# Turning attention probabilities by DMA instead of on TensorE, with each attention spread over two sets of products

## The chip, the cores and the metric

The kernel runs on one core of one Trainium2 chip. The metric is the device time of one execution, in microseconds (us). TensorE (PE) multiplies matrices into PSUM, VectorE (DVE), ScalarE (ACT) and GpSimd (POOL) work elementwise, and SyncE (SP) issues every DMA of this kernel. Each engine runs its own instructions in the order in which the program issued them, and waits on semaphores for the others.

## The reference

Input `x` is 128 graphs of 64 nodes with 768 features, with a boolean 64x64 mask per graph. Two layers follow one another, each `x = layernorm(x + f(x, adj))`, all in float32.

```python
# layer 0: 12 heads of 64, additive attention, gate
h = einsum('bnd,ade->bane', x, W); th = tanh(h)
attn = leaky(th @ w_src + swap(th @ w_dst)); masked softmax
feat = elu(attn @ h + b); gate = sigmoid(x @ H_w.T + H_b)
f0 = gate * feat + (1 - gate) * x
# layer 1: 6 heads of 128, dot-product attention
q, k, v = heads(x @ Wq + bq), heads(x @ Wk + bk), heads(x @ Wv + bv)
probs = softmax(q @ k.T / sqrt(128) + bias(adj))
f1 = merge(probs @ v) @ Wf + bf
```

The change is in layer 1, in what stands between `probs` and `probs @ v`.

## The kernel before, in words

**Tiles.** A tile is 128 rows, that is two graphs. 64 tiles make 32 pairs, and 16 groups of two pairs (four tiles). A weight of 768x768 is cut in 2x2 blocks, and a product of two 2x2 block matrices is done with seven block products (a `Job`, lines 199 to 247): `product(i)` issues three matrix products of 128 rows into a PSUM bank, and `way_out(i)` evicts or adds the bank. `step` (L257) issues the product of one step and then the ways out of the step before it. Some products accumulate onto a bank that an earlier way out has to have read first: 6, 7, 4 and 3 do (L212), which follows from the seven-product scheme.

**Stages.** The first half of the program (up to L977) does layer 0 and also layer 1's values `v`, which go to DRAM (`v_d`), as do the layer's result by rows (`x1_d`) and by features (`x1T_d`). The second half (from L980) goes over 16 groups. In each group there are three sets of query and key products, one for each feature column `fc` of 128 (two heads: `fc` and `fc + 3`), and then the output products of the group before. A set is 14 steps in the order `WOVEN` (L46), two jobs interleaved. Query and key steps have 256 columns, output steps 384.

**The order of the work around the change.** It is written out by hand with generators. `woven` (L513) issues a step and then advances each side generator by one `yield`; `drain` runs a generator to its end. `attention` (L345) is one such side: it loads values (eight DMAs, L354), and then, `yield` by `yield`: scores on PE into a bank `sp` (L366), bias and maximum on DVE (L375, L383), subtraction (L385) and exponential on ACT (L386), row sum and division on DVE (L390 to L393), the transposes on PE into a bank `sT` (L398), their copy into `scT` on ACT (L403), context products on PE into two banks `cp` (L414), and their eviction by ACT into `ctxT` (L427). The attention of `(g, fc)` is created after set `(g, fc)` and advanced in the next set, where it ends. PSUM banks with the tag `m` (scores, transposes, context products) number two. Other sides are `residuals` (L436: loads `x1_d`, adds the bias on POOL and forms the block sums of `ctxT` on DVE), `finish` (L497: layer norm and output of the pairs two output sets back) and, in the first group, `last_weight` (L986: the output weight's four blocks, and their sums on DVE). `load_group` (L300) loads the next group's `x1T_d` blocks and forms their four sums on POOL; it is called after the third set of each group.

**PE** needs, in a query or key job, that ACT (ways out of products 1, 6, 7 and 4, L338 and L340) and DVE (products 2, 7 and 3, L339) have read the bank. In output jobs all ways out are on DVE (L481).

Of the kernel before, what the change touches and what calls it, by code (L numbers as in the profile page):

```python
# [8 lines left out]

F32 = mybir.dt.float32  # L10
U8 = mybir.dt.uint8
AF = mybir.ActivationFunctionType
ALU = mybir.AluOpType
AX = mybir.AxisListType

P = 128
# [3 lines left out]
HK = KC // 2  # L20
# [11 lines left out]
GT = 4  # L32
# [58 lines left out]
def kernel(  # L91
# [21 lines left out]
    nc = tc.nc  # L113
# [13 lines left out]
    def bank(tag, name, bufs=2):  # L127
        return ps.tile([P, 512], F32, tag=tag, name=name, bufs=bufs)
# [3 lines left out]
    x1T_d = [dram.tile([P, KC, PAIR * P], F32, name=f"x1Td_{p}") for p in range(NP)]  # L132
    v_d = [dram.tile([P, D], F32, name=f"vd_{t}") for t in range(2 * NP)]
    dst_d = [dram.tile([P, H0], F32, name=f"dstd_{t}") for t in range(2 * NP)]


    ident = const.tile([P, P], F32, name="ident")
# [157 lines left out]
    def query_tiles(g, fc):  # L295
        qk[g, fc] = [
            pools["early"].tile([P, 2, GT * P], F32, tag=f"{k}T", name=f"{k}T_{g}_{fc}") for k in "qk"
        ]

    def load_group(g, eng, between=lambda: None):  # L300

        pool = pools["early"]
        sums = sum_tiles(pool, "sq", W2, f"q{g}")
        between()
        blocks = {}
        for m, kh in ((0, 0), (1, 0), (1, 1), (0, 1)):
            t = pool.tile([P, HK, W2], F32, tag=f"a{m}{kh}", name=f"a{m}{kh}_{g}", bufs=1)
            nc.sync.dma_start(out=t, in_=x1T_d[2 * g + m][:, kh * HK : (kh + 1) * HK, :])
            blocks[m, kh] = t
        groups[g], steps = block_sums(eng, sums, *(blocks[m, kh] for m in range(2) for kh in range(2)))  # L310
        return steps

    def feature_jobs(g, fc):
# [28 lines left out]

    ctxT = {}

    def attention(g, fc, bias):  # L345

        sb = pools["late"]
        qT, kT = qk.pop((g, fc))

        v = sb.tile([P, GT, 2, E1], F32, tag="v1", name=f"v1_{g}_{fc}")  # L350
        for a in range(2):
            c0 = (a * J1 + fc) * E1
            for i in range(GT):
                nc.sync.dma_start(  # L354
                    out=v[a * N : (a + 1) * N, i, :, :],
                    in_=v_d[GT * g + i][:, c0 : c0 + E1].rearrange("(g m) e -> m g e", m=N),
                )
        yield
        yield
        yield  # L360
        sp = bank("m", f"sp_{g}_{fc}")
        for i in range(GT):
            for a in range(2):
                for gr in range(2):
                    at = slice(i * P + gr * N, i * P + (gr + 1) * N)
                    T.matmul(  # L366
                        sp[gr * N : (gr + 1) * N, (i * 2 + a) * N : (i * 2 + a + 1) * N],
                        qT[:, a, at],
                        kT[:, a, at],
                        start=True,  # L370
                        stop=True,
                    )
        yield
        sc = sb.tile([P, GT, 2, N], F32, tag="sc", name=f"sc_{g}_{fc}")
        V.tensor_tensor(  # L375
            sc,
            sp.rearrange("p (i a m) -> p i a m", i=GT, a=2),
            bias.unsqueeze(2).to_broadcast([P, GT, 2, N]),
            ALU.add,
        )  # L380
        sc3 = sc.rearrange("p i a m -> p (i a) m")
        mx = small.tile([P, 2 * GT], F32, tag="mx1", name=f"mx1_{g}_{fc}")
        V.tensor_reduce(mx, sc3, AX.X, ALU.max)  # L383
        yield
        V.tensor_tensor(sc3, sc3, mx.unsqueeze(2).to_broadcast([P, 2 * GT, N]), ALU.subtract)  # L385
        S.activation(sc, sc, AF.Exp, scale=SCALE)  # L386
        yield
        yield
        den = small.tile([P, 2 * GT], F32, tag="den1", name=f"den1_{g}_{fc}")
        V.tensor_reduce(den, sc3, AX.X, ALU.add)  # L390
        rden = small.tile([P, 2 * GT], F32, tag="rden1", name=f"rden1_{g}_{fc}")
        V.reciprocal(rden, den)
        V.tensor_tensor(sc3, sc3, rden.unsqueeze(2).to_broadcast([P, 2 * GT, N]), ALU.mult)  # L393
        yield
        yield
        sT = bank("m", f"sT_{g}_{fc}")
        for i in range(GT):
            T.transpose(  # L398
                sT[:, i * P : (i + 1) * P], sc[:, i].rearrange("p a m -> p (a m)"), ident
            )  # L400
        yield
        scT = sb.tile([P, GT * P], F32, tag="scT", name=f"scT_{g}_{fc}")
        S.copy(scT, sT)  # L403
        yield
        yield
        cp = [bank("m", f"cp_{g}_{fc}_{a}") for a in range(2)]
        for i in range(GT):
            for gr in range(2):
                at = slice(i * P + gr * N, i * P + (gr + 1) * N)
                for a in range(2):  # L410
                    rows = slice(a * N, (a + 1) * N)
                    for half in range(2):
                        e = slice(half * N, (half + 1) * N)
                        T.matmul(  # L414
                            cp[a][e, at], v[rows, i, gr, e], scT[rows, at], start=True, stop=True
                        )
        yield
        if g not in ctxT:
            ctxT[g] = [
                sb.tile([P, KC, W2], F32, tag="ctxT", name=f"ctxT_{g}_{pr}", bufs=4)  # L420
                for pr in range(2)
            ]

        for a in range(2):
            hd = a * J1 + fc
            for pr in range(2):
                S.activation(  # L427
                    ctxT[g][pr][:, hd, :],
                    cp[a][:, pr * W2 : (pr + 1) * W2],
                    AF.Identity,  # L430
                    bias=bias_c["v"][:, hd : hd + 1],
                )
# [80 lines left out]
    def woven(pair, *sides, order=WOVEN):  # L513

        for k, i in order:
            step(pair[k], i)
            for s in sides:
                next(s, None)

    def drain(*sides):  # L520
        for s in sides:
# [458 lines left out]
    with ExitStack() as ph:  # L980
        sb = pools["late"] = ph.enter_context(
            tc.tile_pool(name="sb1", bufs=2, reuse_waits="tile")
        )
        nothing = iter(())

        def last_weight():  # L986

            weights["f"] = load_weight(wf, "wc", "wf")
            pools["bf"] = sb.tile([P, D], F32, name="bf_bc", bufs=1)
            nc.sync.dma_start(out=pools["bf"], in_=bf.partition_broadcast(P))  # L990
            for s in weight_sums(V, weights["f"]):
                for _ in range(3):
                    yield
                s()

        adjs[0] = load_adj(sb, 0, GT, "adjg_0")
        biases = {0: mask_bias(0)}
        attend, done = attention(0, 0, biases[0]), nothing
        next(attend)
        for g in range(NG):  # L1000
            last = g == NG - 1
            rows = residuals(g - 1, False) if g > 0 else last_weight()
            for fc in range(HK):
                if (g, fc) == (0, 0):
                    continue
                if fc == 1 and not last:
                    adjs[g + 1] = load_adj(sb, GT * (g + 1), GT, f"adjg_{g + 1}")
                if fc == 2 and not last:
                    biases[g + 1] = mask_bias(g + 1)
                if (g, fc) == (0, 1):  # L1010
                    pair, order = (jobs["Q"], jobs["K"]), LAST_REST
                else:
                    query_tiles(g, fc)
                    pair, order = feature_jobs(g, fc), WOVEN
                sides = [attend] + [done] * (fc == 0) + [rows] * (fc == 2)
                woven(pair, *sides, order=order)
                drain(*sides)
                attend = attention(g, fc, biases[g])
                next(attend)
            if not last:  # L1020
                all_of(load_group(g + 1, G))
            if g > 0:
                pair = out_job(2 * g - 2), out_job(2 * g - 1)
                if last:
                    attend = chain(attend, residuals(g, True))
                woven(pair, *[attend] * (1 + last))
                drain(attend)
                attend = nothing
                done = finish(2 * g - 2, 2 * g - 1)
        p = 2 * NG - 2  # L1030
        pair = out_job(p), out_job(p + 1)
        woven(pair, done, done, order=ENDS[:9])
        drain(done)
        done = finish(p)
        woven(pair, done, done, order=ENDS[9:-1])
        n0, n1 = norm(p + 1, 0), norm(p + 1, 1, last_half=0)
        step(pair[1], ENDS[-1][1])
        next(n0)
        next(n1)
        drain(done)  # L1040
        flush()
        next(n0, None)
        next(n1)
        next(n1, None)
# [42 lines left out]
```

## Time and profile before

| | |
|---|---|
| median of 3 runs | 2967.19 us (2966.39 to 2970.22) |
| profiled execution, its own time | 2970.77 us |
| its span, first to last instruction | 2969.0 us |
| PE busy in the span | 2925.2 us, 99% |
| DVE, ACT, POOL busy | 1796.9, 1009.0, 811.1 us |
| granted TensorE clock | 0.995 |
| one group of layer 1 (2089.96 to 2180.46 in the trace) | 90.50 us, PE busy 90.50 |

The profile is of one execution. "Busy" is the time in which an engine worked on data; the issuing of DMAs is not counted in it. A line of the groups names the line of the kernel, the engine, the operation, what it writes and reads, the shape, the count, then busy us and mean ns of one, and the idle time before it with what ended it. A line of the timeline gives the start and the length in us, the engine and the instruction. PE's matmuls overlap, so what one costs in a stream is read from start to start.

### The profile page before, as it was taken

What the parts mean: (1) busy time and instruction counts of PE and PEld (TensorE: products, weight loads), DVE (VectorE), ACT (ScalarE), POOL (GpSimd) and SP (SyncE); (2) the same over time, 40 slices, a digit from 0 to 9 for tenths busy, and PEclk for the clock granted to TensorE, in tenths of its full rate; (3) what the DMA queues carried; (4) which work ended last, traced back from release to release, by engine and by line L of the source; (5) the groups of instructions that cost most, each with busy time, mean ns of one, the idle gap of its engine ahead of it and who ended that gap; (6) DMA issues with size and microseconds to landing.
All of it is one profiled execution on the core that took longest, in us unless ns stands there. A gap on an engine that the chain in (4) does not pass through costs nothing.

```text
span 2969.0 us, 45314 instructions
## 1 busy us (share of the span) xinstructions
PE 2925.2 (99%) x18048; PEld 2023.0 (68%) x18048; DVE 1796.9 (61%) x3017; ACT 1009.0 (34%) x1761; POOL 811.1 (27%) x650
## 2 busy tenths in 40 slices
PE   7999999999999999999999999999999999999999
PEld 4566666666666666666578777787777887777875
DVE  6878888788788878887844344333343443443345
ACT  2344344444443444444422222222222222222221
POOL 2434333333343333333422212211111212121121
PEclk9999999999999999999999999999999999999999
DMA  5333333334333333343532211222212222112221
GB/s 171 122 109 114 107 121 115 103 118 128 104 119 104 121 113 106 115 129 103 176 97 77 70 60 55 86 86 76 68 52 64 86 76 73 59 57 82 87 80 48
DMA packets 179681, 284.81 MB, mean 96 GB/s; under 512 B 46736, under 2 KB 113296, under 8 KB 179472
## 3 DMA queue, kind: packets, MB, share of 16 engines
q1 hardware_dynamic: 179472, 281.93, 29.1%
q8 instruction: 143, 2.34, 0.3%
q14 instruction: 66, 0.54, 0.1%
HBM read 167.81 MB, written 101.06 MB: 91 GB/s over the span
## 4 chain that ended last, share of the span: by engine, by line
PE 94%; DVE 3%; DMA 1%; ACT 1%; issue 0%; SPq 0%; POOLq 0%; POOL 0%; DVEq 0%; ACTq 0%
PE y_k L222 8%; PE y_o L222 8%; PE y_q L222 8%; PE y_v L222 8%; PE y_h L222 8%; PE y_g L222 8%; PE z_v L222 4%; PE z_o L222 4%; PE z_k L222 4%; PE z_h L222 4%; PE z_q L222 4%; PE z_g L222 4%; PE x_k L222 2%; PE x_o L222 2%; PE x_q L222 2%; PE x_h L222 2%
## 5 line engine op out<-in xcount | busy, mean ns | idle before, releaser
L789 POOL TENSOR_TENSOR x<-gate,x 128x768 f32<-128x768 f32 x64 | 117.4, 1835 | 323.8 <-ACT gate L840 309.0
L457 POOL TENSOR_TENSOR y<-y,bf_bc 128x768 f32<-128x768 f32 x64 | 115.3, 1832 | 311.4 <-DMA y<-x1d 311.4
L481 DVE TENSOR_TENSOR y<-y_o,y 128x384 f32<-128x384 f32 x128 | 71.4, 557 | 202.1 <-PE y_o L222 198.0
L339 DVE TENSOR_TENSOR kT<-z_k,kT 128x256 f32<-128x256 f32 x96 | 40.8, 425 | 239.3 <-PE z_k L222 136.1
L662 POOL TENSOR_TENSOR th<-th,wsd 128x768 f32<-128x768 f32 x64 | 117.2, 1832 | 182.5 <-DVE th L661 182.5
L274 POOL TENSOR_TENSOR rs_b<-ve_b,minus_half 128x1 f32<-128x1 f32 x64 | 35.1, 548 | 452.5 <-DVE ve_b L272 451.7
L192 POOL TENSOR_TENSOR sq_q<-a,a 128x768 f32<-128x768 f32 x16 | 29.2, 1828 | 432.8 <-PE y_o L222 286.9
L222 PE MATMUL y_h<-w_wq,xT 128*128 128x384 f32 x384 | 136.3, 492 | 8.6 <-DMA w_wq<-in_w_dram 7.9
L222 PE MATMUL y_k<-a,hw_wk 128*128 128x256 f32 x576 | 144.6, 387 | 0.0
L222 PE MATMUL y_q<-a,w_wq 128*128 128x256 f32 x576 | 140.9, 381 | 1.9 <-ACT qT L338 1.9
L222 PE MATMUL z_v<-wv,sv_v 128*128 128x384 f32 x384 | 138.9, 498 | 3.2 <-DVE v L652 3.2
L222 PE MATMUL y_q<-sq_q,w_wq 128*128 128x256 f32 x576 | 140.3, 380 | 0.9 <-ACT qT L338 0.9
L222 PE MATMUL y_h<-w_wq,sx_x 128*128 128x384 f32 x384 | 136.5, 492 | 4.2 <-ACT h L622 4.2
L222 PE MATMUL z_q<-sq_q,w_wq 128*128 128x256 f32 x576 | 140.1, 379 | 0.0
L222 PE MATMUL y_k<-sq_q,hw_wk 128*128 128x256 f32 x576 | 140.1, 379 | 0.0
L222 PE MATMUL z_k<-sq_q,hw_wk 128*128 128x256 f32 x576 | 140.0, 379 | 0.0
L338 ACT ACTIVATE qT<-y_q,bq_c 128x256 f32<-128x256 f32 x144 | 67.4, 469 | 213.2 <-PE y_q L222 213.2
L222 PE MATMUL y_v<-wv,sv_v 128*128 128x384 f32 x384 | 136.6, 492 | 3.0 <-DVE sv_v L193 3.0
L386 ACT ACTIVATE sc<-sc 128x512 f32<-128x512 f32 x48 | 30.2, 630 | 319.3 <-DVE sc L385 319.3
L222 PE MATMUL z_h<-w_wq,sx_x 128*128 128x384 f32 x384 | 137.6, 495 | 0.9 <-DVE w_wq L168 0.9
L222 PE MATMUL y_g<-hw_wk,sx_x 128*128 128x384 f32 x384 | 134.9, 488 | 2.4 <-DVE hw_wk L171 2.2
L222 PE MATMUL y_v<-wv,x1T 128*128 128x384 f32 x384 | 136.1, 491 | 1.2 <-ACT x1T L739 1.0
(171 smaller groups left out, 6678.1 us busy)
## 6 DMA issues: line engine op xcount, KB each, us to landing
x<-in_x_dram SPq DMA_DIRECT2D x64, 384.0 KB, 3.6
dd<-dstd SPq DMA_DIRECT2D x128, 192.0 KB, 3.4
x1d<-x SPq DMA_DIRECT2D x64, 384.0 KB, 2.6
x1Td<-x1T SPq DMA_DIRECT2D x32, 768.0 KB, 4.8
vd<-v SPq DMA_DIRECT2D x64, 384.0 KB, 2.9
a<-x1Td SPq DMA_DIRECT2D x64, 384.0 KB, 3.6
v<-vd SPq DMA_DIRECT2D x384, 64.0 KB, 2.3
y<-x1d SPq DMA_DIRECT2D x64, 384.0 KB, 4.1
```

The source lines that it names most:

```text
L192: lambda: e.tensor_tensor(s1, a21, a22, ALU.add),
L222: T.matmul(to[:, : self.n], lhsT, rhs, start=kc == 0 and not more, stop=kc == HK - 1, skip_group_check=more,)
L274: G.tensor_tensor(rstd, ve, minus_half, ALU.pow)
L338: lambda mn, bk_: S.activation(at(*mn), bk_, AF.Identity, bias=bias(mn[1])),
L339: lambda mn, bk_: V.tensor_tensor(at(*mn), bk_, at(*mn), ALU.add),
L386: S.activation(sc, sc, AF.Exp, scale=SCALE)
L457: G.tensor_tensor(y, y, pools["bf"], ALU.add)
L481: V.tensor_tensor(at(*mn), b, at(*mn), ALU.add)
L662: G.tensor_tensor(th[:, 1, :], th[:, 1, :], wsd[:, 1, :], ALU.mult)
L789: G.tensor_tensor(xp, st[t]["gate"], xp, ALU.mult)
```

## The change

All attentions of layer 1 but the last no longer turn their probabilities on PE. A float32 word is taken as two 16-bit halves. ACT copies the low halves and the high halves of the probabilities apart into `scT`'s memory; a DMA stores both to DRAM (`halves_d`, two buffers that take turns); two DMA transposes, one for each half, read them back turned into the memory of `sc`; and ACT joins the halves again into `scT`. The last attention still transposes on PE.

The new steps have more `yield`s between them, so an attention is advanced over two sets: its scores, softmax and the start of the DMAs in the first, the joining copies, context products and their evictions in the second (`older` and `attend` in the loop). The output set and the first query/key set of the next group thus carry the second halves of attentions that the sets before began.

Other edits go with it. The output weight's blocks are loaded two steps apart, and their sums come after the loads. Three of group 1's `x1T_d` blocks are loaded with them, ahead of `load_group`. Two of group 1's four sums go to DVE, and these sums are a side of the next set.

```diff
+    halves_d = [dram.tile([2, GT, P, P], U16, name=f"halvesd_{i}") for i in range(2)]
...
+    of_x1T = {}
+
+    def load_x1T(g, m, kh):
+        t = pools["early"].tile([P, HK, W2], F32, tag=f"a{m}{kh}", name=f"a{m}{kh}_{g}", bufs=1)
+        nc.sync.dma_start(out=t, in_=x1T_d[2 * g + m][:, kh * HK : (kh + 1) * HK, :])
+        of_x1T[g, m, kh] = t
...
-        blocks = {}
         for m, kh in ((0, 0), (1, 0), (1, 1), (0, 1)):
-            t = pool.tile([P, HK, W2], F32, tag=f"a{m}{kh}", name=f"a{m}{kh}_{g}", bufs=1)
-            nc.sync.dma_start(out=t, in_=x1T_d[2 * g + m][:, kh * HK : (kh + 1) * HK, :])
-            blocks[m, kh] = t
-        groups[g], steps = block_sums(eng, sums, *(blocks[m, kh] for m in range(2) for kh in range(2)))
+            if (g, m, kh) not in of_x1T:
+                load_x1T(g, m, kh)
+        groups[g], steps = block_sums(eng, sums, *(of_x1T.pop((g, m, kh)) for m in range(2) for kh in range(2)))
...
-    def attention(g, fc, bias):
+    def attention(g, fc, bias, by_dma=True):
...
-        yield
-        yield
-        sT = bank("m", f"sT_{g}_{fc}")
-        for i in range(GT):
-            T.transpose(
-                sT[:, i * P : (i + 1) * P], sc[:, i].rearrange("p a m -> p (a m)"), ident
-            )
-        yield
         scT = sb.tile([P, GT * P], F32, tag="scT", name=f"scT_{g}_{fc}")
-        S.copy(scT, sT)
-        yield
-        yield
+        if by_dma:
+            yield
+            apart, turned = (
+                t.bitcast(U16).rearrange("p (h e) -> p h e", h=2)
+                for t in (scT, sc.rearrange("p i a m -> p (i a m)"))
+            )
+            words, wordsT = (
+                t.bitcast(U16).rearrange("p (e h) -> p h e", h=2)
+                for t in (sc.rearrange("p i a m -> p (i a m)"), scT)
+            )
+            for h in range(2):
+                S.copy(apart[:, h], words[:, h])
+            yield
+            dr = halves_d[(g * HK + fc) % 2]
+            nc.sync.dma_start(
+                out=dr.rearrange("h i p c -> p h i c"),
+                in_=apart.rearrange("p h (i c) -> p h i c", c=P),
+            )
+            yield
+            yield
+            yield
+            for h in range(2):
+                nc.sync.dma_start_transpose(
+                    out=turned[:, h], in_=dr[h].rearrange("i p c -> (i p) c")
+                )
+            yield
+            yield
+            yield
+            for h in range(2):
+                S.copy(wordsT[:, h], turned[:, h])
+            yield
+            yield
+            yield
+            yield
+            yield
+        else:
...
+    def in_turn(steps):
+        yield
+        for s in steps:
+            s()
+            yield
...
-            weights["f"] = load_weight(wf, "wc", "wf")
+            weights["f"] = load_weight(wf, "wc", "wf", ())
             pools["bf"] = sb.tile([P, D], F32, name="bf_bc", bufs=1)
+            for block in (B11, B21, B22, T3):
+                yield
+                yield
+                load_block(wf, weights["f"], block)
+            load_x1T(1, 0, 0)
+            load_x1T(1, 0, 1)
+            load_x1T(1, 1, 0)
             nc.sync.dma_start(out=pools["bf"], in_=bf.partition_broadcast(P))
             for s in weight_sums(V, weights["f"]):
-                for _ in range(3):
-                    yield
+                yield
                 s()
...
-        attend, done = attention(0, 0, biases[0]), nothing
+        attend, older, done = attention(0, 0, biases[0]), nothing, nothing
...
-                sides = [attend] + [done] * (fc == 0) + [rows] * (fc == 2)
-                woven(pair, *sides, order=order)
+                sides = [older] + [done] * (fc == 0) + [rows] * (fc == 2)
+                woven(pair, *sides, attend, order=order)
                 drain(*sides)
-                attend = attention(g, fc, biases[g])
+                older, attend = attend, attention(g, fc, biases[g], not (last and fc == 2))
                 next(attend)
             if not last:
-                all_of(load_group(g + 1, G))
+                sums = load_group(g + 1, G if g else (V, G))
+                if g:
+                    all_of(sums)
+                else:
+                    done = in_turn(sums)
             if g > 0:
                 pair = out_job(2 * g - 2), out_job(2 * g - 1)
                 if last:
                     attend = chain(attend, residuals(g, True))
-                woven(pair, *[attend] * (1 + last))
-                drain(attend)
-                attend = nothing
+                woven(pair, older, *[attend] * (1 + last))
+                drain(older)
+                if last:
+                    drain(attend)
+                older, attend = attend, nothing
```

More of the change, by code (lines that the diff above doesn't have):

```diff
@@ L11 @@
 U8 = mybir.dt.uint8
+U16 = mybir.dt.uint16
 AF = mybir.ActivationFunctionType
@@ L393, in attention @@
         V.tensor_tensor(sc3, sc3, rden.unsqueeze(2).to_broadcast([P, 2 * GT, N]), ALU.mult)
-        yield
-        yield
-        sT = bank("m", f"sT_{g}_{fc}")
-        for i in range(GT):
-            T.transpose(
-                sT[:, i * P : (i + 1) * P], sc[:, i].rearrange("p a m -> p (a m)"), ident
-            )
-        yield
-        scT = sb.tile([P, GT * P], F32, tag="scT", name=f"scT_{g}_{fc}")
-        S.copy(scT, sT)
-        yield
-        yield
+        scT = sb.tile([P, GT * P], F32, tag="scT", name=f"scT_{g}_{fc}")
+        if by_dma:
[3 more added lines that the diff above has]
+                for t in (scT, sc.rearrange("p i a m -> p (i a m)"))
+            )
+            words, wordsT = (
[30 more added lines that the diff above has]
+            yield
+            sT = bank("m", f"sT_{g}_{fc}")
+            for i in range(GT):
+                T.transpose(
+                    sT[:, i * P : (i + 1) * P], sc[:, i].rearrange("p a m -> p (a m)"), ident
+                )
+            yield
+            S.copy(scT, sT)
+            yield
+            yield
         cp = [bank("m", f"cp_{g}_{fc}_{a}") for a in range(2)]
@@ L518, in woven @@
                 next(s, None)
+    def in_turn(steps):
+        yield
+        for s in steps:
+            s()
+            yield
     def drain(*sides):
@@ L986, in last_weight @@
         def last_weight():
-            weights["f"] = load_weight(wf, "wc", "wf")
+            weights["f"] = load_weight(wf, "wc", "wf", ())
             pools["bf"] = sb.tile([P, D], F32, name="bf_bc", bufs=1)
+            for block in (B11, B21, B22, T3):
+                yield
+                yield
+                load_block(wf, weights["f"], block)
+            load_x1T(1, 0, 0)
+            load_x1T(1, 0, 1)
+            load_x1T(1, 1, 0)
             nc.sync.dma_start(out=pools["bf"], in_=bf.partition_broadcast(P))
             for s in weight_sums(V, weights["f"]):
-                for _ in range(3):
-                    yield
+                yield
                 s()
```

## The prediction

> **What bounds the kernel now.** I read the page's busy shares and chain first, then the groups of layer 1 by form, then PE's, DVE's and SP's timelines over one group of four tiles, then the waits.
>
> ```profile
> PE 2925.2 (99%) x18048; PEld 2023.0 (68%) x18048; DVE 1796.9 (61%) x3017; ACT 1009.0 (34%) x1761; POOL 811.1 (27%) x650
> ...
> PE 94%; DVE 3%; DMA 1%; ACT 1%; issue 0%; SPq 0%; POOLq 0%; POOL 0%; DVEq 0%; ACTq 0%
> ```
>
> PE is busy 99% and carries 94% of the chain. A busy PE alone proves little, so I look at a stretch: one whole group (an output set, then three query/key sets), and inside it the second query/key set.
>
> ```profile
> 2089.96:2180.46 90.50, 90.50 (x638) 70.62 (x637) 35.99 (x79) 22.92 (x46) 16.48 (x12) 1.00 0.22 71
> ...
> 2138.03:2159.16 21.13, 21.13 (x185) 18.22 (x184) 6.84 (x13) 6.39 (x14) 7.13 (x4) 1.00 0.38 119
> ```
>
> The columns are the length, then PE, PEld, DVE, ACT and POOL busy, the clock, the DMA share, GB/s. PE has no gap in 90.5 us and the full clock; ACT works 22.9 us of it, DVE 36.0, DMA 22%. So here a PE instruction that goes is time that goes, if nothing else gets late. PE's timeline around the part that is removed:
>
> ```profile
> 2148.37 1.46 PE L222 MATMUL y_q<-sq_q,w_wq 128*128 128x256 f32 x6
> 2149.66 1.46 PE L222 MATMUL z_k<-sq_q,hw_wk 128*128 128x256 f32 x6
> 2150.96 0.60 PE L398 MATMUL sT<-ident,sc 128*128 128x128 f32 x4
> 2151.40 1.46 PE L222 MATMUL y_k<-sq_q,hw_wk 128*128 128x256 f32 x6
> ```
>
> From start to start a step costs 1.295 us and the four transposes 0.44 (the printed 0.60 overlaps the next). In the output set they cost 0.44 as well (2108.49 to 2108.93). What DVE and ACT spend around them:
>
> ```profile
> 2147.43 0.69 DVE L393 TENSOR_TENSOR sc<-sc,rden 128x512 f32<-128x512 f32 x1
> ...
> L427 ACT ACTIVATE ctxT<-cp,bv_c 128x256 f32<-128x256 f32 x164 | 64.4, 475 | 138.8 <-PE cp L414 138.8
> ...
> L403 ACT COPY scT<-sT 128x512 f32<-128x512 f32 x42 | 24.6, 586 | 151.5 <-PE sT L398 151.5
> ```
>
> Probabilities are ready 10.09 us after that set's start. Layer 1's two own PE waits stand at its beginning, and the DMA rows price the new transfers:
>
> ```profile
> PE y_q L222 <- ACT qT L338: 2.8, 2, 1.9
> ...
> PE x_q L222 <- DMA a<-x1Td: 1.9, 1, 1.9
> ```
>
> ```profile
> vd<-v SPq DMA_DIRECT2D x64, 384.0 KB, 2.9
> ...
> v<-vd SPq DMA_DIRECT2D x384, 64.0 KB, 2.3
> ...
> adjg<-in_adj_dram SPq DMA_DIRECT2D x16, 32.0 KB, 2.2
> ```
>
> **What the Trainium skill says.** "VectorE: DVE Perf Modes", The three transpose paths, gives 390 ns on TensorE and 1309 ns on the DMA crossbar for one 128x128 two-byte block. Here TensorE's four float32 blocks cost 0.44 us together in a stream, so that is a latency and not a rate; no crossbar transfer is in this trace. "DMA: Bandwidth & Descriptors", Latency and other measured facts, gives an effective 261 GB/s for DMA transposes in one kernel. The same page, Two DMAs through the same engine are not ordered, says that a transfer that reads what another wrote has to wait for its completion; so SP will stand at each transpose until the store has landed.
>
> **The change, part by part.** One attention is 4 tiles and one feature column; there are 48, and all but the last go the new way: 47.
>
> *Removed.* 47 x 4 transposes on PE: 47 x 0.435 = **-20.4 us** on the path that sets the end. Also 47 `scT` copies on ACT (0.586 each), off the path.
>
> *Added on ACT.* Two copies that part the halves and two that join them. Halves are 512 two-byte elements per partition; the nearest row is the 512-element copy, 0.586. Net +3 x 0.586 = 1.76 us per attention, 83 in all, or 5.3 per group beside ACT's 22.9 of 90.5. Hidden in ACT's idle time; what matters is who queues behind them. The parting copies come at step 8 behind the division (10.09 us; step 8 starts at 10.35 with the scores' 1.28), so ACT barely waits; behind them is the eviction of step 8's product, wanted at step 11, 3.9 us after step 8 starts, against 1.17 + 0.47. Covered. If two-byte strided copies took twice 0.586 it still fits.
>
> *Added DMAs.* Per attention one store of 256 KB in 1024 runs of 256 bytes, and two transposes of 128 KB. The store lies between the 384 KB row (2.9 us) and something slower for its short runs; adjg's 512 runs of 64 bytes land in 2.2. I take 3.0 (2.5 to 4). The pair of transposes is not in the trace. Low end: a small transfer's landing, 2.2 us. High end: eight 128x128 blocks one after another by the page's price, 10.5 us. An estimate from the page's 261 GB/s: 262,144 bytes take 1.0 us, with 2.3 for the landing of a small DMA and 0.6 for SP's second issue (eight v loads take SP 5.1 to 6.0 us), **3.9 us**, which I take, since blocks of one instruction should overlap. Store and pair: 6.9 us.
>
> *What waits.* ACT's joining copies stand at step 1 of the next set, in front of that set's evictions. PE's step 5 accumulates on a bank that the first eviction must have read. I split the group's sets: a query/key set is 18.13 us bare (the window 2119.90 to 2138.03), and 1.28 more with each of scores and context products.
> - First attention of a group (second half in a set with scores): the division ends at 10.09 of 19.41 us; step 5 starts at 4 x 1.295 + 1.28 = 6.46, less 0.47 for the eviction and 1.17 for joining: 4.82. The room is 9.32 + 4.82 - 1.17 (parting) = **13.0 us** for store and pair.
> - Third (first half in the output set of 29.5 us, division at 15.04 + 1.28): 13.2 + 3.54 - 1.17 = **15.6**.
> - Second (second half in the output set, where no ACT eviction feeds PE, so only the context products at step 6 count): 8.9 + 12.9 - 2.3 = **19.5**.
>
> 6.9 fits all of them with 6.1 us to spare. The cover is the half set of block products; without it each late microsecond is one on PE, 16 times for the first kind.
>
> *SP's queue.* Three more issues per attention, some 0.6 us each. Behind the transposes, where SP stands for the store, are eight v loads (used a set later), four y loads (before issued at 2145.85, now about 2160, landed by 2165, four POOL additions of 1.83 till 2173, wanted from 2180) and the x1T loads (two were issued at 2162.17, now about 2183; landing 3.6, four POOL sums 7.3, done 2194; wanted near 2210). All late, none too late.
>
> *Start of layer 1.* The weight blocks are issued apart, their sums come at step 10 and not 4, three x1T blocks come early, and two of group 1's sums go to VectorE. That aims at both waits above: 0.9 us of the first at 1559 and 1.9. Against it, 3.8 MB are in flight while the second attention's store and transposes want to pass, and the second sum is wanted at the next set's step 5. I take -1.5 (from -2.8 to +3).
>
> *The end.* In the last output set the context products of two attentions follow one another in step 6 with two PSUM banks of that tag: the second waits for four evictions, 1.57 us. **+1.6**, once. I see no cover for it.
>
> *Context products moved, masks, residual sums:* same work at another step, nothing.
>
> **Sum.** -20.4 - 1.5 + 1.6 = -20.3. The profiled execution took 2970.77 us (span 2969.0), so 2950.5 there; it lies 3.6 over the median of the runs, 2967.19, against which I forecast **2946.9 us**. The likeliest case's own range is 2941 to 2953.
>
> **Rivals.**
> - *The transposes are late* (ends slower). [...] If store and pair take over 13.0 us, ACT stands at step 1 of the third query/key set and PE stops at step 5. The gain is gone at 20.4/16 = 1.3 us over, 14.3 us (pair 11.3 with a store of 3.0). The page's block price, 10.5, gives a total of 13.5: over by 0.5, 8 us, still faster. A quarter more than it (13.1 us, total 16.1) gives 3.1 x 16 + 0.5 x 15 = 57 us: **3004 us**. For it: short runs on both sides, the HBM round trip twice. Against: 22% DMA share and 6 us of room.
> - *Partly hidden*: transposes make their neighbours late (v, y and x1T loads behind them on SP) or evictions slip by some tenths in each set. Half of the gain: **2957 us**. For it: PE runs without any gap, so any slip shows. Against: the listed rooms.
> - *No difference*: a pair near 11 us eats the gain just up, **2966 us**.
> - *The DMA path is not what it says*: it could be that the copies go through more work than one pass; at most ACT's 83 us, inside its idle time, so this has no own time.
>
> **How the numbers follow.** Hidden 0.53, partly hidden 0.15, no difference 0.05, late 0.27. Faster by over 0.2% is 0.68, within 0.2% 0.05, slower 0.27; 0.2% (5.9 us) is about what a measurement of this kernel can tell from no change. A range that leaves out 2 in 10 runs from 2940 (under it only if the start gains fully) to 2990, which holds the smaller half of the late cases; 2941 to 2953 stands beside it for the likeliest.
>
> **What would show it.** Right: an output-to-output period of 90.5 - 3 x 0.435 = 89.2 us with PE without gap, no `sT` but in the last attention, joining copies on ACT that start at once in step 1, the two waits at 1559 and 1574 smaller. Late: PE waits on ACT's `qT` in the third query/key set of each group, ACT on a DMA into `sc`. Partly: short PE waits on `ctxT`, `kT` or `y`. The prediction is wrong if the pair takes over 11 us, if a transpose holds SP so long that the x1T sums come late, or if PE spends the removed 0.44 us elsewhere.

## The result and the profile after

The changed kernel takes 3004.78 us (median of 4 runs, 3001.74 to 3011.7); the kernel before, run beside it, 2968.68. The ratio is 1.0126, with a 95% interval of 1.0113 to 1.0138: slower by 36 us, where 20 us less had been forecast. The profiled execution took 3001.74 us, with a span of 2999.9.

The page of the changed kernel first: the busy shares and the chain.

```profile
PE 2915.2 (97%) x17860; PEld 2007.5 (67%) x17860; DVE 1886.1 (63%) x3019; ACT 1095.7 (37%) x1902; POOL 830.3 (28%) x648
...
PE 88%; DVE 8%; ACT 2%; DMA 1%; SPq 1%; issue 0%; POOL 0%; POOLq 0%; DVEq 0%; ACTq 0%
```

PE is busy for 10 us less than before (2925.2), and the span is 30.9 us longer: PE now stands idle for 84.7 us, 40.9 more than before. DVE's busy time has grown by 89 us, though DVE was given nearly the same instructions (3019 instead of 3017). DVE's share of the chain went from 3% to 8%. So something made DVE's instructions longer.

PE's waits in layer 1 (the view of waits from 1535 us on; columns: who waited for whom, us in all, how often, longest):

```profile
PE y_q L225 <- ACT qT L346: 33.3, 20, 2.2
PE y_q L225 <- DVE sq_q L196: 8.3, 1, 8.3
PE cp L460 <- ACT ctxT L473: 1.3, 2, 0.9
```

Of the first, 15 are waits of some 2 us, one in the third set of each group but group 0, and five are short ones (0.2 to 0.6 us) in the same sets. The other two lines are the start and the end of layer 1. One group in windows: from output set to output set, and below it the third query/key set alone.

```profile
2103.70:2196.15 92.45, 89.72 (x626) 69.29 (x625) 43.34 (x79) 28.66 (x56) 18.01 (x12) 1.00 0.28 87
...
2172.18:2196.15 23.97, 21.24 (x182) 17.67 (x181) 15.97 (x20) 7.81 (x18) 8.21 (x4) 1.00 0.35 104
```

The group takes 92.45 us; the mean of 13 groups is 92.19 (from 1642.65 to 2841.06), where before it was 90.50. The first two query/key sets have the forecast 19.41 us. The third should have 20.69 (19.41 and 1.28 for the context products that it also carries) and has 23.97, with PE busy 21.24. Its timeline on PE:

```profile
2182.42 1.56 PE L225 MATMUL z_q<-sq_q,w_wq 128*128 128x256 f32 x6
2184.56 1.56 PE L225 MATMUL y_q<-sq_q,w_wq 128*128 128x256 f32 x6 [0.58 <-ACT qT L346]
2185.96 1.46 PE L225 MATMUL z_k<-sq_q,hw_wk 128*128 128x256 f32 x6
2187.25 1.46 PE L225 MATMUL y_k<-sq_q,hw_wk 128*128 128x256 f32 x6
2190.86 1.56 PE L225 MATMUL y_q<-a,w_wq 128*128 128x256 f32 x6 [2.15 <-ACT qT L346]
```

There are two waits for an eviction by ACT, of 0.58 and 2.15 us; from start to start they cost 3.1 (2.14 in place of 1.40, and 3.61 in place of 1.295). What held ACT, in ACT's timeline:

```profile
2189.30 1.14 ACT L416 COPY scT<-sc 128x512 uint16<-128x512 uint16 x2 [2.97 <-DVE sc L401]
2190.34 0.47 ACT L346 ACTIVATE qT<-y_q,bq_c 128x256 f32<-128x256 f32 x1
```

The parting copies waited 2.97 us for DVE's division, and the eviction that PE needed stood behind them. And what held DVE, in DVE's timeline with POOL's one line of that stretch:

```profile
2178.09 0.69 DVE L391 TENSOR_REDUCE mx<-sc 128x8 f32<-128x512 f32 x1
...
2179.25 2.00 DVE L196 TENSOR_TENSOR so_o<-so_o,ctxT 128x384 f32<-128x384 f32 x1
2181.18 2.30 DVE L393 TENSOR_TENSOR sc<-sc,mx 128x512 f32<-128x512 f32 x1
2183.40 2.17 DVE L197 TENSOR_TENSOR so_o<-ctxT 128x384 f32<-128x384 f32 x1
2185.49 2.16 DVE L198 TENSOR_TENSOR so_o<-ctxT,so_o 128x384 f32<-128x384 f32 x1
2187.57 0.67 DVE L398 TENSOR_REDUCE den<-sc 128x8 f32<-128x512 f32 x1
...
2188.52 0.69 DVE L401 TENSOR_TENSOR sc<-sc,rden 128x512 f32<-128x512 f32 x1
...
2179.03 8.21 POOL L503 TENSOR_TENSOR y<-y,bf_bc 128x768 f32<-128x768 f32 x4 [35.45 <-DMA y<-x1d]
```

Four DVE instructions with two inputs in SBUF (L196, L393, L197 and L198) take 8.6 us. In the kernel before, the same four of a third set take 2.3:

```profile
2166.47 0.68 DVE L385 TENSOR_TENSOR sc<-sc,mx 128x512 f32<-128x512 f32 x1
2167.07 0.55 DVE L193 TENSOR_TENSOR so_o<-so_o,ctxT 128x384 f32<-128x384 f32 x1
2167.54 0.55 DVE L194 TENSOR_TENSOR so_o<-ctxT 128x384 f32<-128x384 f32 x1
...
2169.57 0.55 DVE L195 TENSOR_TENSOR so_o<-ctxT,so_o 128x384 f32<-128x384 f32 x1
```

The slow ones lie exactly beside POOL's four additions of the output bias to the residual rows. These additions were in the second set before, after that set's division. Here is POOL's line of the kernel before:

```profile
2149.37 7.13 POOL L457 TENSOR_TENSOR y<-y,bf_bc 128x768 f32<-128x768 f32 x4 [19.25 <-DMA y<-x1d]
```

The set there ran from 2138.03 to 2159.16. What moved the additions is seen on SP. Before:

```profile
2139.77 5.99 SPq L354 DMA_DIRECT2D v<-vd  x8
2145.85 1.96 SPq L450 DMA_DIRECT2D y<-x1d  x4
```

And after, with the second set running from 2152.77 to 2172.18:

```profile
2164.12 0.40 SPq L419 DMA_DIRECT2D halvesd<-scT  x1
2166.77 2.45 SPq L427 DMA_TRANSPOSE sc<-halvesd  x2
2169.31 6.09 SPq L362 DMA_DIRECT2D v<-vd  x8
2175.44 2.02 SPq L496 DMA_DIRECT2D y<-x1d  x4
```

SP issues its DMAs in the order of the program. The y loads now stand behind the store (which waits for ACT's copies), the transposes (which wait for the store) and eight v loads. They are issued 22.7 us after the second set's start, where it was 7.8 before.

The Trainium skill names such a collision. "SBUF — State Buffer", Who interferes with whom, says that a DVE instruction with two SBUF inputs contends with a GpSimd instruction that reads SBUF, that whichever issues first holds the port pair they share for its whole length while the other waits, and that `tensor_reduce` never contends on this chip. The trace agrees: two-input instructions went from 0.55 and 0.68 to 2.0 to 2.3 us. No reduction of this stretch lies beside POOL's additions; in the seventh experiment two do, and they keep their 0.69. The runs below show whether this makes the loss.

The two spans differ by 30.9 us, and that is the sum of four parts. In 13 groups the transposes that are gone save 1.32 us each and the waits add 3.01 (92.19 against 89.18, the period of experiment 4), which makes -17.2 and +39.1. The stretch up to the first output set is 5.2 us longer (1642.65 against 1637.45). The end, from output set number 14 on, is 3.8 longer (158.84 against 155.02); it holds the waits of one more group.

### The profile page after: what moved, and what is told of

Its sections match the earlier page's. It is cut to its first block, busy times and chain, and to the rows that moved or that the text cites. A ratio compares the mean times of both kernels' runs of the same rounds, so it can differ in the third digit from the quotient of the medians.

```text
span 2999.9 us, 45190 instructions
## 1 busy us (share of the span) xinstructions
PE 2915.2 (97%) x17860; PEld 2007.5 (67%) x17860; DVE 1886.1 (63%) x3019; ACT 1095.7 (37%) x1902; POOL 830.3 (28%) x648
## 4 chain that ended last, share of the span: by engine, by line
PE 88%; DVE 8%; ACT 2%; DMA 1%; SPq 1%; issue 0%; POOL 0%; POOLq 0%; DVEq 0%; ACTq 0%
PE y_o L225 8%; PE y_v L225 8%; PE y_h L225 8%; PE y_g L225 8%; PE y_q L225 7%; PE y_k L225 7%; PE z_o L225 4%; PE z_v L225 4%; PE z_h L225 4%; PE z_g L225 4%; PE z_q L225 4%; PE z_k L225 3%; PE x_k L225 2%; PE x_o L225 2%; PE x_q L225 2%; PE x_h L225 2%
## 5 line engine op out<-in xcount | busy, mean ns | idle before, releaser
L503 POOL TENSOR_TENSOR y<-y,bf_bc 128x768 f32<-128x768 f32 x64 | 130.6, 2071 | 546.0 <-DMA y<-x1d 504.1
L225 PEld LDWEIGHTS y_q<-a,w_wq 128*128 128x128 f32 x576 | 110.3, 194 | 56.9 <-ACT qT L346 38.8
L347 DVE TENSOR_TENSOR qT<-z_q,qT 128x256 f32<-128x256 f32 x96 | 40.8, 425 | 164.6 <-ACT qT L346 101.1
L713 DVE TENSOR_TENSOR th<-th,wsd 128x768 f32<-128x768 f32 x64 | 67.6, 1056 | 108.7 <-ACT th L712 108.7
```

The costliest lines, as they stand in the source:

```text
L225: T.matmul(to[:, : self.n], lhsT, rhs, start=kc == 0 and not more, stop=kc == HK - 1, skip_group_check=more,)
L347: lambda mn, bk_: V.tensor_tensor(at(*mn), bk_, at(*mn), ALU.add),
L503: G.tensor_tensor(y, y, pools["bf"], ALU.add)
L713: V.tensor_tensor(th[:, 0, :], th[:, 1, :], wsd[:, 0, :], ALU.mult)
```

## The experiments

Ratios are to the kernel before, with a 95% interval.

**1. POOL's additions taken away, all else as changed.**

```diff
-                G.tensor_tensor(y, y, pools["bf"], ALU.add)
+                if last:
+                    G.tensor_tensor(y, y, pools["bf"], ALU.add)
```

> The changed kernel without POOL's additions of the output bias to the residual rows (left out for groups 0 to 14; the rest is untouched). The theory: in each third query/key set POOL's four additions (8.2 us) now run beside DVE's softmax and block sums, whose instructions then take 2.0 to 2.3 us instead of 0.55 to 0.69; so the division ends some 5 us later, ACT's parting copies wait for it, and PE waits for the evictions queued behind them. It expects the period of a group to fall from 92.2 to 89.2-89.5 us, PE's waits for ACT in the third sets to vanish, and about 2961 us. Rival: the late y loads or the crossbar transposes themselves slow SBUF's readers, or ACT's extra copies do it; then the loads, transposes and copies are still there and the period stays at 91.5-92.5, about 3000 us.

This kernel leaves the output bias out in all groups but the last. Measured: 2957.99 us, ratio 0.9964 (0.9952 to 0.9977). A group:

```profile
2083.96:2173.16 89.20, 89.20 (x625) 69.46 (x624) 36.45 (x80) 28.49 (x56) 10.15 (x8) 1.00 0.29 90
```

PE is without a gap, and the period is the forecast 89.2. The late y loads, the store, the transposes and ACT's four copies are all still there. So none of them costs anything by itself in the groups, and the rival named there falls.

**2. The collision alone, put into the kernel before.** POOL's additions wait for the third set's row maxima.

```diff
-            for y in ys[2 * g + pr]:
+            for y in ys[2 * g + pr] if last else ():
...
+                if not last and (pr, k) == (0, 1):
+                    gate = small.tile([P, 2 * GT], F32, tag="hold", name=f"hold_{g}")
+                    G.tensor_tensor(gate, latest["mx"], latest["mx"], ALU.add)
+                    for y in ys[2 * g] + ys[2 * g + 1]:
+                        G.tensor_tensor(y, y, pools["bf"], ALU.add)
```

> The kernel before, with the same additions on POOL held back until the third set's row maxima are there (one small POOL instruction of 8 columns reads them); nothing else is changed. The theory: the collision alone makes the loss, without any transpose by DMA. DVE's instructions in the third set rise to about 2 us, the division ends about 5 us later than 10.5 us after the set's start, and PE's own transposes, with 2.4 us to spare, wait 2 to 3 us per group: 14 to 15 groups, about 3000 to 3010 us. Rival: the collision needs the new DMAs; then about 2968 us.

Measured: 3032.82 us, ratio 1.0219 (1.0204 to 1.0234). No transpose by DMA is in this kernel. Its third set, DVE and PE:

```profile
2094.41 2.13 DVE L387 TENSOR_TENSOR sc<-sc,mx 128x512 f32<-128x512 f32 x1
...
2103.06 0.93 PE L400 MATMUL sT<-ident,sc 128*128 128x128 f32 x4 [2.59 <-DVE sc L395]
2103.78 2.77 PE L222 MATMUL y_k<-sq_q,hw_wk 128*128 128x256 f32 x6
2106.34 1.62 PE L222 MATMUL y_q<-a,w_wq 128*128 128x256 f32 x6
```

The wait of 2.6 us per group is as expected (38.8 in all), but the time is 23 us over the range. After the wait the transposes take 0.72 us from start to start in place of 0.44, and the next step 2.56 in place of 1.295; the granted clock is 0.53 there (2103.06 to 2106.40) and was 1.00 before the wait. Most groups take 95.2 us in place of 90.5, that is 4.7 us for a wait of 2.6. The expectation had counted the wait alone. The collision alone is enough, and it hurts more here, where PE waits for the division itself.

**3. All attentions turned on PE again, the rest as changed.** The very first attention, which is created ahead of the loop, still goes by DMA.

```diff
-                older, attend = attend, attention(g, fc, biases[g], not (last and fc == 2))
+                older, attend = attend, attention(g, fc, biases[g], False)
```

> The changed kernel with every attention turned on PE as before; the new start of layer 1 and the new order of the sides stay. The theory: the y loads are early again, POOL's additions fall in the second set, the period is 90.5 us again; what differs from the kernel before is the start of layer 1 alone: 2965 to 2973 us. Rival: the new order of the sides (attention last in each step) or the start itself costs the larger part: 2985 us or more.

Measured: 2964.17 us, ratio 0.9986 (0.998 to 0.9993), just under the expected range. The period is 90.5 again (2718.04 to 2808.54 from output set to output set), and the first output set begins 5.4 us earlier than in the kernel before. So the edits to the start, taken without the DMAs (but for the first attention's), are a gain of some 4.5 us, and the order of the sides costs nothing.

**4. The repair on SP.** The y loads are issued at the start of the second set, ahead of its store; POOL's additions wait for that set's reciprocals.

```diff
+    def add_bias(g):
+        hold = small.tile([P, 2 * GT], F32, tag="hold", name=f"hold_{g}")
+        G.tensor_tensor(hold, latest["rden"], latest["rden"], ALU.add)
+        for y in ys[2 * g] + ys[2 * g + 1]:
+            G.tensor_tensor(y, y, pools["bf"], ALU.add)
...
+                if fc == 1 and g > 0:
+                    load_ys(g - 1, False)
                 sides = [older] + [done] * (fc == 0) + [rows] * (fc == 2)
                 woven(pair, *sides, attend, order=order)
                 drain(*sides)
+                if fc == 1 and g > 0:
+                    add_bias(g - 1)
```

> The changed kernel with the y loads issued at the start of each second query/key set, ahead of that set's store and transposes, and POOL's additions held until the division of that set is nearly done (a small POOL instruction reads the reciprocals), so that they run in a stretch where DVE mostly reads PSUM. All of the computation is there. The theory: the same gain as without the additions, period 89.2-89.6 us, about 2961 us, which is below the kernel before; what stays is the stall at the start of layer 1. Rival (DMA traffic or ACT): about 3000 us.

Measured: 2958.83 us, ratio 0.9969 (0.9958 to 0.998). With all of the computation it is as fast as without the additions. One group, and POOL's additions in it:

```profile
2085.96:2175.15 89.19, 89.19 (x626) 69.46 (x625) 37.91 (x79) 28.66 (x56) 17.95 (x13) 1.00 0.30 90
...
2145.00 7.13 POOL L504 TENSOR_TENSOR y<-y,bf_bc 128x768 f32<-128x768 f32 x4
```

POOL's additions take 7.13 us again. The block sums on DVE begin 6.7 us after their end, at 2158.78, and take 0.55 each. This kernel is 46 us faster than the changed one, with the same DMAs in another order and POOL's additions at another time.

**5. The parting copies three steps later.**

```diff
             yield
+            yield
+            yield
+            yield
...
             for h in range(2):
                 S.copy(apart[:, h], words[:, h])
-            yield
             dr = halves_d[(g * HK + fc) % 2]
```

(One `yield` fewer before the transposes, and one fewer before the context products, so that these stay at step 20.)

> The changed kernel with the two parting copies three steps later (step 11 and not 8; store in the same step, transposes at 13, joining copies at 16, context products at 20 as they are); POOL's additions still collide. The theory says that PE does not wait for DVE but for the evictions that ACT holds behind the parting copies; three steps later these evictions are ahead of them: of about 2.7 us of PE waits in each third set (0.6 behind the exponential, 2.1 behind the copies) some 0.6 to 1 stay, and the time falls by 25 to 35 us to 2968-2980. Rival: DVE's own late additions onto the query and key tiles or a late context stage hold PE; then 2995 to 3010 us.

Measured: 2953.16 us, ratio 0.9952 (0.9937 to 0.9967), better than expected, and for a reason that I had not thought of. The second set's store moved too, the y loads with it, and POOL's additions now begin after the third set's division (2071.32, the division at 2070.50 to 2071.19). Two causes changed at once; this run tells nothing about ACT's queue. Hence number 8. A group takes 89.18 us as in number 4. The traces put the 6.3 us by which this kernel's span is shorter than number 4's at the start (the first output set begins 4.6 us earlier) and at the end (1.7, where PE no longer waits for the last attention's division).

**6. The start of layer 1 in another order**, with the repair of number 4: the output weight's blocks are issued before the first attention's store, three of group 1's x1T blocks after the second attention's store, the fourth before the next v loads, the bias row last.

```diff
+            for _ in range(9):
+                yield
+            load_x1T(1, 0, 0)
+            load_x1T(1, 0, 1)
+            load_x1T(1, 1, 0)
             for s in weight_sums(V, weights["f"]):
-                yield
                 s()
+                yield
+            load_x1T(1, 1, 1)
...
                 if (g, fc) == (0, 1):
+                    weights["f"] = load_weight(wf, "wc", "wf")
```

> The kernel with early y loads and held additions (2958.8 us), and the start of layer 1 put in another order: the output weight's four blocks are issued before the first attention's store, three x1T blocks of group 1 after the second attention's store, the fourth before the next v loads, the bias row last. All of the computation is there. The theory of the 8 us stall there: the second attention's store takes 9.2 us to land behind 3.8 MB of loads, SP stands at its transposes meanwhile, and the eight v loads and then the last x1T block come after it. Expected 2947 to 2951 us. Rival: the stall is the DVE sums' own length or the load's; then 2956 to 2960 us.

Measured: 2948.62 us, ratio 0.9936 (0.9921 to 0.9951), as expected. In the changed kernel SP shows the stall that went:

```profile
1557.29 0.39 SPq L419 DMA_DIRECT2D halvesd<-scT  x1
1566.83 2.45 SPq L427 DMA_TRANSPOSE sc<-halvesd  x2
1569.39 5.15 SPq L362 DMA_DIRECT2D v<-vd  x8
1574.64 0.54 SPq L307 DMA_DIRECT2D a<-x1Td  x1
```

The store landed after 9.2 us behind the weight, x1T and bias loads (2.6 elsewhere); SP stood until 1566.83; the last x1T block was issued at 1574.64; DVE's sums waited for it and PE for them, 8.26 us. With the new order that wait is gone from PE's list, and the first output set begins 9.6 us earlier than in number 4.

**7. Early y loads, additions not held.**

```diff
     def add_bias(g):
-        hold = small.tile([P, 2 * GT], F32, tag="hold", name=f"hold_{g}")
-        G.tensor_tensor(hold, latest["rden"], latest["rden"], ALU.add)
```

> The kernel with early y loads, but POOL's additions start as soon as the rows are there, that is about where the second set's softmax runs on DVE. If what counts is only that the additions are not beside the block sums, it equals the held version, 2959 us. If what counts is whether they meet DVE instructions that have all operands in SBUF, three softmax instructions of the second set (subtraction, and after the exponential the division) take over 2 us, the division comes some 3 us later, ACT's copies with it, and PE waits 0 to 2 us per group: 2959 to 2985 us, with instructions of over 1 us in the second set and none in the third.

Measured: 2963.52 us, ratio 0.9984 (0.9977 to 0.9991), 4.7 us slower than number 4. The second set's softmax now meets POOL's additions:

```profile
2142.16 8.03 POOL L502 TENSOR_TENSOR y<-y,bf_bc 128x768 f32<-128x768 f32 x4 [14.84 <-DMA y<-x1d]
...
2142.42 0.69 DVE L392 TENSOR_REDUCE mx<-sc 128x8 f32<-128x512 f32 x1
2143.59 0.93 DVE L394 TENSOR_TENSOR sc<-sc,mx 128x512 f32<-128x512 f32 x1
2145.22 0.69 DVE L399 TENSOR_REDUCE den<-sc 128x8 f32<-128x512 f32 x1 [0.70 <-ACT sc L395]
...
2146.18 2.34 DVE L403 TENSOR_TENSOR sc<-sc,rden 128x512 f32<-128x512 f32 x1
```

The two reductions keep their 0.69 us inside POOL's work. The two-input division takes 2.34, the subtraction only 0.93, so one instruction and not three took over 2 us. Nine of the 14 groups are 0.6 to 1.0 us longer than 89.19, each with a wait of 0.4 us for ACT; with one of 1.4 at the start these are 5.1 us in all. Where the collision falls decides: with few two-input instructions beside POOL it costs a tenth of what it cost in the changed kernel (4.7 us and 46).

**8. The parting copies later for the second attention of each group alone**, so that the y loads and the collision stay in place. (`late = fc == 1` in the edit of number 5.)

> The changed kernel with the parting copies three steps later for the second attention of each group alone, the one whose softmax lies in the third set; the first attention's store stays where it is, so the y loads and POOL's additions should stay beside the third set's softmax as in the changed kernel (in the version that moved all copies the y loads came later as well, which left two causes in one run). If PE is held by evictions queued on ACT behind the copies that wait for the division, 0.6 to 1 us of 2.7 us per third set stays although DVE's instructions still take over 2 us: 2962 to 2975 us. If the late DVE itself holds PE, the waits stay: 2990 us or more.

Measured: 2964.75 us, ratio 0.9987 (0.9979 to 0.9994). The collision is there (DVE is busy for 1880.2 us, nearly the 1886.1 of the changed kernel), the long wait is not:

```profile
2072.72 1.93 DVE L196 TENSOR_TENSOR so_o<-so_o,ctxT 128x384 f32<-128x384 f32 x1
2074.57 2.30 DVE L393 TENSOR_TENSOR sc<-sc,mx 128x512 f32<-128x512 f32 x1
2076.79 2.16 DVE L197 TENSOR_TENSOR so_o<-ctxT 128x384 f32<-128x384 f32 x1
...
2077.95 1.56 PE L225 MATMUL y_q<-sq_q,w_wq 128*128 128x256 f32 x6 [0.51 <-ACT qT L346]
```

The 2.15 us wait behind the copies is gone, and the period is 89.70 (1638.35 to 2804.46, 13 groups). So the late DVE reached PE through ACT's queue: of the 3.0 us that it cost per group, 2.5 went with the copies' place, and 0.5 stays. In four groups the trace shows what stays as a wait of 0.35 to 0.51 us behind the exponential, on ACT as well; in the others no wait is recorded.

**9 and 10. Combinations.** Number 9 is later copies for all attentions with the start of number 6, without the change to the y loads; number 10 is number 6 with the later copies of number 8.

> The changed kernel with all parting copies three steps later (2953.2 us) and the reordered start of layer 1 (2948.6 us with the other fix). The two act in different places, so their gains should add: the 6.8 us wait and its slow clock at the start go, 2943 to 2947 us. If not, the start reorder does not fit the later copies and it stays at 2950 to 2954 us.

> All three repairs: early y loads with held additions, later parting copies in the third set alone, reordered start. As POOL's additions are then clear of the third set, the later copies have nothing left to repair: the same as with early y loads and reordered start, 2947 to 2950 us.

Measured: 2949.16 us, ratio 0.9936 (0.9921 to 0.9951), and 2949.10, ratio 0.9935 (0.992 to 0.9949). Number 9 misses its range by 2 us: PE still waits 3.5 us for ACT and 1.9 for a DVE sum, once each, around the start of layer 1. Number 10 is number 6 again, as expected. The three versions at 2949 can't be told apart; each is about 0.64% faster than the kernel before.

## Why the prediction was wrong

- **Transposes gone from PE: right.** -20.4 us by 0.435 each; numbers 1 and 4 have 89.18 to 89.20 us per group against a forecast of 89.2.
- **Store and pair of transposes: right, and the late rival was not what happened.** The store landed in 2.6 us (3.0 taken), a transpose 2.5 us after its issue, with 1.245 of SP's time each (0.6 taken). From the store's issue to the second landing it is some 6.4 us, where 6.9 was taken and the rooms were 13.0 to 19.5. That the rival's time, 3004, equals the result is chance: its place was right (the third set, PE behind ACT's `qT`), its mechanism was not: it had ACT wait for a DMA, and ACT waited for DVE's division. In numbers 1 and 4 the transposes are as they were, and no wait is left in the groups.
- **ACT's copies: size a little off, conclusion right.** 0.617 for parting and 0.764 for joining, with 0.586 taken.
- **SP's queue: the step that failed.** "All late, none too late". The y loads were seen to move behind the transposes, and even POOL's additions were placed well, into the first part of the third set. Then they were judged only by when their result is wanted, and their cost was put at nothing. What they run beside was not asked: DVE's block sums and softmax, with two inputs in SBUF, which take 8.6 us there in place of 2.3. That costs 3.0 us per group, 39 in 13 groups, against a forecast gain of 1.3 per group. Number 2 shows that moving the additions there is enough for a loss, number 4 that moving them back removes it.
- **"Behind them is the eviction of step 8's product ... Covered": failed with it.** The cover of 2 us was worked out for a division at 10.1 us after the set's start. In the third set it ended at 17.0 (2189.21 against 2172.18), while number 4 has 10.7 there (2165.00 against 2154.29). Number 8 shows that this queue is how the delay got to PE.
- **Start of layer 1: wrong by size.** -1.5 was taken, with +3 as the worst. The wait was 8.26 us, and the steps after it ran slowly. The store behind 3.8 MB was named, but it was not carried on through SP: store, transposes, eight v loads and only then the last x1T block. Number 3 shows -4.5 for the same edits without the DMAs, number 6 about -10 against number 4.
- **The end: the banks about right, another wait missed.** +1.6 was taken for the banks, and PE waited 1.3 for them. In numbers 1 and 4 PE waits another 1.6 for the division of the last attention, which was put at nothing; the changed kernel does not show that wait.
- **The chances.** Nothing between "partly hidden" and "the transposes are late" stood for a collision of two engines that the moved transfers bring about, though the partly hidden case had its seed, late neighbours behind the transposes.

## What to carry to other kernels

When a transfer moves in a queue, follow it to the instruction that it starts, and ask not only when its result is wanted but also what runs beside it on other engines: GpSimd beside two-input SBUF instructions of VectorE made those four times as long. On an engine whose evictions feed TensorE, an instruction that may have to wait should stand behind those evictions, not ahead of them: here that was worth 2.5 us of the 3.0 per group. A store whose completion SP has to wait for delays everything behind it on SP; here it landed in 2.6 us in the groups and in 9.2 where large loads had been issued just before.

## What the runs showed of the hardware that was not expected

- Two-input DVE instructions on SBUF operands took 2.0 to 2.3 us beside POOL's additions in the changed kernel, about one addition each, while two reductions beside them kept 0.69 (number 7). POOL's additions rose from 1.78 to 2.05 us (7.13 and 8.21 for four).
- After some PE waits the granted clock was low for about two steps, so a wait can cost PE more than its length. In 3 of the 13 groups of the changed kernel it was 0.57 over the 4 us after a wait of 1.94 to 2.04 us, and the group took 93.1 us; in the ten others, after waits of 1.95 to 2.16 us, the next step ran as usual, and the group took 91.4 to 92.5. So the length of the wait alone did not decide it, and what did stays open. After the 8.26 us wait a step of 1.295 us took 2.69, at a clock of 0.53. A step of each kind in the changed kernel:

```profile
2190.86 1.56 PE L225 MATMUL y_q<-a,w_wq 128*128 128x256 f32 x6 [2.15 <-ACT qT L346]
...
2557.64 2.88 PE L225 MATMUL y_q<-a,w_wq 128*128 128x256 f32 x6 [1.94 <-ACT qT L346]
```

- A transpose of 512x128 two-byte words from DRAM, 128 KB, costs 1.245 us of SP's time and lands 2.5 us after its issue (medians of 94; 2.3 to 4.3 to landing).
